# Local attention layers: one slot for both key tiles of a unit, a new queue order on ScalarE, the last norm moved into the feed-forward half, offsets added on VectorE

## The chip, the cores and the metric

The kernel runs on one core of a Trainium2 chip. The metric is the device time of one execution in microseconds (us). A core has a matrix engine (TensorE, PE in the profile, with its weight loads as PEld), VectorE (DVE), ScalarE (ACT), GpSimd (POOL) and a queue of its own for DMAs (SP). Each engine runs its own instructions in order and waits for the others by semaphores.

## The reference, cut to what matters

A network of sixteen blocks over 16 sequences of 256 tokens with 128 channels. Two of the blocks, `_L0_ffn_ref`, are made of two local layers each, so the kernel computes four local layers. One of them:

```python
def _layer(x, wqkv, qs, ksc, wo, lg, lb, w1, b1, w2, b2):
    h = shift_token(x)                     # half of the channels from the token before
    q, k, v = split(h @ wqkv)              # 8 heads of 64
    q = l2norm(q) * qs
    k = l2norm(k) * ksc
    q, k = rotary_xpos(q, k)
    # softmax over keys j with i - 64 <= j <= i, scores times 8
    o = local_attention(q, k, v)
    x = x + o @ wo
    h = shift_token(x)
    h = (h - mean(h)) / sqrt(var(h) + 1e-05) * lg + lb
    a, g = split(h @ w1 + b1)
    return x + (a * gelu(g)) @ w2 + b2
```

The performer block (`_L0_attn_b_ref`) ends its two halves with norms of the same form, with a gain and an offset.

## The kernel before, in words

The activations lie transposed, 128 channels by 4096 tokens: `x` is the residual stream, `z` (tile `ha`) a local layer's running sum, `hs` (tile `hb`) its shifted copy. A chunk is 512 tokens (two sequences; 8 chunks, `NCH`), a tile 128 tokens (32 tiles, `NTILE`).

`local_attend` handles a layer's attention. Its steps:

- `project(n)`: PE multiplies a tile of `hs` by the q and k weights into two banks of PSUM ("w"). ACT squares them into `sq`, DVE multiplies them by tables of cosines and sines into `t1` and `t2` (four products, `t<-ps,tab`).
- `rotate(n)`: DVE sums the squares (`ss`) and takes a maximum; POOL adds `t1` and `t2` crosswise (`t<-t,t`, two instructions).
- `unit(n)`: ACT turns `ss` into an inverse length (Ln, then Exp); POOL multiplies `t1` by it (`t<-t,ss`).
- `turn(n)`: PE transposes q and k (eight transposes, two "w" banks), ACT copies them into `qkt`; PE makes v (a third "w" bank), ACT copies it.
- `score`: products of keys and queries. A sequence has two tiles of keys: the first (`t` = 0) is seen by 192 queries, the second (`t` = 1) by 128. A unit is one sequence (`b`) and half of its heads (`hg`, four heads), so there are 32 units. Of the first key tile DVE masks the scores by a minimum with `see`, and ACT takes the exponential of 768 columns at once; of the second a bfloat16 product of `identb` and `masked` adds the mask on PE, and ACT takes the exponentials out of PSUM.
- `weigh`: 24 products of 32 columns: the weights' sums (`pd`, products with ones) and the weighted values (`po`). ACT then makes the inverse of `pd` (`rd`: Ln, then Exp).
- `divide`: DVE multiplies `po` by `rd` into `ot`.
- `out(c)`: four products with `wo`; DVE adds them to `z`.
- `chunk_steps`: the norm of `x` ahead of the first layer (for chunks that the stage before has not normalised already), the shifts on POOL, and for each chunk the second half's norm: `centre_step` (a PE product, ACT's copy, POOL's squares `nsq`), `spread_step` (a PE product, ACT's Ln and Exp into `nrs`), and `scale` (DVE `scalar_tensor_tensor` with the gain, ACT `Identity` with the offset).

`local_ffn` does the second half: `wide` (six products into "f" banks, Gelu on ACT, products on DVE), `narrow` (three products into a "z" bank).

The order on every engine is written out by hand (`manual_schedule`): a loop over slots `k`, two slots per key tile pair, calls the steps each with its own offset; there is no planner. Slot `k` scores one key tile of one unit and weighs the one of two slots earlier; `project` runs ten slots ahead of the tile's number times two, `out` follows ten slots later. PSUM has eight banks, shared as three "w", two "s" (scores) and three "o" (`pd` and `po`). All small operations go through helpers, so that the profile shows their lines: L504 matmul, L508 transpose, L528 ACT, L531 DVE tensor_tensor, L534 POOL, L538 and L540 DVE tensor_scalar, L543 DVE scalar_tensor_tensor; L3478 is weigh, L3406 the sum of squares.

Of the kernel before, what the change touches and what calls it, by code (L numbers as in the profile page):

```python
# [1649 lines left out]
class Fast(Net):  # L1650
# [140 lines left out]
    def norm_steps(self, pool, src, dst, bank, g=None, b=None, eps="eps5", copy=None, square=False):  # L1791


        held = {}

        def centre():
            held[0] = self.centre_step(pool, src, dst, bank, copy, square)

        def spread():
            held[1] = self.spread_step(pool, held[0], bank, eps)  # L1800

        def scale():
            if g is None:
                self.tt(dst, dst, held[1], ALU.mult)
            else:
                self.stt(dst, dst, g, held[1], ALU.mult, ALU.mult)
                self.act(dst, dst, AF.Identity, bias=b)

        return [centre, spread, scale]

# [1549 lines left out]
    def local_attend(self, w, z, hs, last):  # L3360

        nc = self.nc
        with ExitStack() as st:
            p = self.stage(st, "l1", 1)
# [9 lines left out]
            masked = one([P, P], "masked", BF16)  # L3377
            self.ts(masked, w["see"][:, :P], 0.0, ALU.min)
            identb = one([P, P], "identb", BF16)
            nc.vector.tensor_copy(identb, self.ident)  # L3380
            least = one([P, 16], "least")
            nc.gpsimd.memset(least, 1e-24)
            made, rot, qkt, val, weights, sums, outs, steps = {}, {}, {}, {}, {}, {}, {}, {}

            def project(n):
                s = slice(n * P, n * P + P)
# [26 lines left out]
            def unit(n):  # L3413
                t1, ss = rot[n]

                self.act(ss, ss, AF.Ln, scale=2.0**20)
                self.act(ss, ss, AF.Exp, scale=-0.5)
                t3 = t1.rearrange("p i h a d -> p (i h) (a d)")
                self.gt(t3, t3, ss[:, :, None].broadcast_to([P, 16, 64]), ALU.mult)
# [13 lines left out]
                val[n] = p.tile([P, 512], F32, tag="v", name="v", bufs=6)  # L3433
                self.act(val[n], pv, AF.Copy)

            def score(b, hg, t):
                wide = 192 - 64 * t
                qt, kt = qkt[b][:, 0], qkt[b][:, 1]
                ps = [self.bank("s"), self.bank("s")]
                pt = p.tile([P, 2, 384], F32, tag="pt", name="pt", bufs=4)  # L3440
                if t:
                    for a in range(2):
                        self.mm(ps[a][:, :T], identb, self.twice(masked), stop=False)
                for i in range(2):
                    g = 2 * hg + i
                    for a in range(2):
                        rows = slice(64 * a, 64 * a + 64)
                        self.mm(
                            ps[a][:, i * wide : i * wide + wide], kt[rows, g, t * P : t * P + P],
                            qt[rows, g, t * P : t * P + wide], start=t == 0, stop=t == 0 or i == 1,  # L3450
                        )
                if t:
                    for a in range(2):
                        self.act(pt[:, a, :T], ps[a][:, :T], AF.Exp)
                else:
                    for a in range(2):
                        self.tt(
                            pt[:, a].rearrange("p (i t) -> p i t", i=2), ps[a][:, :384].rearrange("p (i t) -> p i t", i=2),
                            self.twice(w["see"]), ALU.min,
                        )  # L3460
                    flat = pt.rearrange("p a t -> p (a t)")
                    self.act(flat, flat, AF.Exp)
                weights[b, hg, t] = pt

            def weigh(b, hg, t):


                wide = 192 - 64 * t
                if t == 0:
                    sums[b, hg] = self.bank("o"), self.bank("o")  # L3470
                pt = weights.pop((b, hg, t))
                pd, po = sums[b, hg]
                for half in range(-1, 2):
                    for r in range(4):
                        i, a = divmod(r, 2)
                        d = (4 * hg + r) * 64 + 32 * half
                        at = max(half, 0) * T + t * P
                        nc.tensor.matmul(  # L3478
                            (pd if half < 0 else po)[32 * r : 32 * r + 32, at : at + wide],
                            self.ones64[:, :32] if half < 0 else val[2 * b + t][:, d : d + 32],  # L3480
                            pt[:, a, i * wide : i * wide + wide], start=t == 0 and half < 1, stop=t == 1 and half != 0,
                            skip_group_check=True,
                        )
                if t == 1:
                    del sums[b, hg]
                    rd = p.tile([P, T], F32, tag="rd", name="rd", bufs=2)
                    self.act(rd, pd[:, :T], AF.Ln)
                    self.act(rd, rd, AF.Exp, scale=-1.0)
                    sums[b, hg] = po, rd

            def divide(b, hg):
                if b % 2 == 0 and hg == 0:
                    outs[b // 2] = p.tile([P, 4, CH], F32, tag="ot", name="ot", bufs=1)
                po, rd = sums.pop((b, hg))
                at = b % 2 * T
                self.tt(
                    outs[b // 2][:, 2 * hg : 2 * hg + 2, at : at + T], po.rearrange("p (g t) -> p g t", g=2),
                    self.twice(rd), ALU.mult,
                )
# [6 lines left out]
                zs = z[:, self.chunk(c)]  # L3506
                self.tt(zs, zs, pz, ALU.add)

            def at(k, slot, every, many):

                n, rest = divmod(k - slot, every)
                return n if rest == 0 and 0 <= n < many else None

            def chunk_steps(k):
                if not last:
                    for i, slot in enumerate((-17, -15, -13)):
                        if (c := at(k, slot, 8, NCH)) is not None:
                            self.norm_x_step(p, c, i, "w")
                for slot in (-12, 11):
                    if (c := at(k, slot, 8, NCH)) is not None:  # L3520
                        self.shift(hs[:, self.chunk(c)], z[:, self.chunk(c)])
                for i, slot in enumerate((12, 14, 16)):
                    if (c := at(k, slot, 8, NCH)) is not None:
                        if i == 0:
                            s = hs[:, self.chunk(c)]
                            steps[1] = self.norm_steps(p, s, s, "w", w["lg"], w["lb"])
                        steps[1][i]()

            with self.share(w=3, s=2, o=3), self.tc.manual_schedule():
                self.logs()  # L3530
                units = [(b, hg, t) for b in range(B) for hg in range(2) for t in range(2)]
                for k in range(-17, len(units) + 17):
                    if k % 2 == 0 and 0 <= k - 4 < len(units):
                        divide(*units[k - 4][:2])
                    if (n := at(k, -7, 2, NTILE)) is not None:
                        unit(n)
                    if 0 <= k < len(units):
                        score(*units[k])
                    if 0 <= k - 2 < len(units):
                        weigh(*units[k - 2])  # L3540
                    if (n := at(k, -10, 2, NTILE)) is not None:
                        project(n)
                    if (n := at(k, -9, 2, NTILE)) is not None:
                        rotate(n)
                    if (n := at(k, -5, 2, NTILE)) is not None:
                        turn(n)
                    if (c := at(k, 10, 8, NCH)) is not None:
                        out(c)
                    chunk_steps(k)

    def local_ffn(self, w, z, hn, last):
        with ExitStack() as st:
            p = self.stage(st, "l3", 2)
# [22 lines left out]

            lead = self.lead(p, "z", tables=True) if last else []
            with self.share(f=6, z=2), self.tc.manual_schedule():
                for k in range(NCH + 1 + len(lead)):
                    if k < NCH:  # L3580
                        wide(k)
                    if 0 < k <= NCH:
                        narrow(k - 1)
                    for i in reversed(range(len(lead))):
                        if 0 <= (c := k - 2 - i) < NCH:
                            lead[i](c)
# [221 lines left out]
```

## Time and profile before

| what | us |
|---|---|
| median of 3 runs (4367.05 to 4376.58) | 4374.96 |
| the profiled execution, its own time | 4392.96 |
| its span | 4391.2 |
| PE busy | 3966.2 |
| DVE busy | 2605.3 |
| ACT busy | 2376.1 |
| POOL busy | 2119.4 |
| first to last score, layers 1 to 4 | 272.8, 259.3, 272.8, 259.6 |
| unit to unit in layer 2, a repeating group of four | 7.42, 12.03, 8.28, 8.28 |

The profile is of one execution, whose time stands beside its span. In a row of the timeline the columns are the start, the time from its first to its last instruction, the engine, the line, the operation, what it writes and reads, its form, the count, and in brackets the idle time of the engine before it and what ended it. A matmul in 32-bit floats stands as two instructions. In a row of busy times by stretch come the stretch, its length, then PE, PEld, DVE, ACT and POOL with their counts, the granted clock, the DMA share and GB/s. In a group of four units one unit holds the out projection (12.03), one the centre step and one the spread step of the norm (8.28 each), and one neither (7.42).

### The profile page before, as it was taken

To read this page: it belongs to the slowest core of one execution; us is meant where nothing else is said; L and a number is where in the kernel's file an instruction comes from. 1 tells how busy PE (TensorE), PEld (TensorE's weight loads), DVE (VectorE), ACT (ScalarE), POOL (GpSimd) and SP (SyncE) were. 2 spreads that over 40 slices of the span, in tenths; PEclk is the share of its full clock that TensorE was granted. 3 is DMA by queue.
4 is the path that set the end of the run, shared out by engine and by line. 5 is a ranking of instruction groups with operands and counts; after the bars stand their busy time and mean duration, and the time that the engine had idled before them with its cause. 6 is when DMAs were issued, how large, how long until landed. Compare 5 with 4: busy or idle time off the path is not lost. (4 is left out here: it accounts for less than half of the span.)

```text
span 4391.2 us, 72802 instructions
## 1 busy us (share of the span) xinstructions
PE 3966.2 (90%) x28390; PEld 2202.4 (50%) x28390; DVE 2605.3 (59%) x4455; ACT 2376.1 (54%) x4549; POOL 2119.4 (48%) x1776
## 2 busy tenths in 40 slices
PE   7899999999899999995989969887999899899978
PEld 3455455466355445543975549643333344355333
DVE  4764566364366377456336643564888788386374
ACT  6665466444766456553447634445555554675442
POOL 4653355232455255315433334466998789521251
PEclk8999999999999999997999979998999999999989
DMA  1800000000000000001940029200000000000000
GB/s 59 332 1 1 11 1 1 19 1 1 19 1 1 1 3 1 1 0 49 310 162 10 15 88 326 86 18 16 1 1 1 3 1 1 15 2 18 6 0 20
DMA packets 78400, 176.36 MB, mean 40 GB/s; under 512 B 12606, under 2 KB 39108, under 8 KB 77920
## 3 DMA queue, kind: packets, MB, share of 16 engines
q1 hardware_dynamic: 65568, 148.40, 9.8%
q0 software_dynamic: 9120, 18.51, 1.2%
q8 instruction: 227, 3.72, 0.4%
q10 hardware_dynamic: 3360, 4.72, 0.3%
q14 instruction: 125, 1.02, 0.1%
HBM read 118.28 MB, written 54.20 MB: 39 GB/s over the span
## 5 line engine op out<-in xcount | busy, mean ns | idle before, releaser
L528 ACT ACTIVATE pt<-ps 128x512 f32<-128x512 f32 (+1 forms) x896 | 423.1, 537 | 408.1 <-PE ps L504 406.8
L504 PE MATMUL ps<-hb,w 128*128 128x512 f32 (+1 forms) x960 | 468.9, 623 | 5.4 <-issue 3.3
L531 DVE TENSOR_TENSOR t<-ps,tab 128x512 f32<-128x512 f32 x512 | 319.3, 683 | 196.1 <-ACT sq L528 191.3
L504 PE MATMUL ps<-w,hb 128*128 128x512 f32 (+2 forms) x896 | 415.1, 576 | 13.6 <-DVE t L531 11.3
L534 POOL TENSOR_TENSOR t<-t,ss 128x1024 f32<-128x1024 f32 x128 | 243.7, 1904 | 306.8 <-ACT ss L528 197.7
L534 POOL TENSOR_TENSOR t<-t,t 128x512 f32<-128x512 f32 x256 | 320.5, 1275 | 13.2 <-PE ps L504 10.1
L504 PEld LDWEIGHTS ps<-hb,w 128*128 128x128 f32 (+1 forms) x960 | 183.6, 196 | 273.5 <-issue 247.3
L531 DVE TENSOR_TENSOR u<-u,ps 128x384 f32<-128x384 f32 (+1 forms) x206 | 121.8, 595 | 277.8 <-ACT u L528 131.2
L534 POOL TENSOR_TENSOR nsq<-ha 128x512 f32<-128x512 f32 x112 | 123.2, 1100 | 314.1 <-ACT ha L528 297.3
L504 PE MATMUL ps<-nsq,ct 128*128 128x512 f32 x368 | 209.5, 654 | 53.9 <-POOL nsq L534 35.0
L528 ACT ACTIVATE pt<-pt 128x768 f32<-128x768 f32 (+1 forms) x160 | 169.5, 1060 | 154.6 <-DVE pt L531 154.6
L2199 POOL DMA_INDIRECT back<-y,x x142 | 139.1, 980 | 184.2 <-ACT y L528 90.2
L504 PE MATMUL ps<-qkt 64*128 64x192 f32 (+1 forms) x2048 | 216.2, 326 | 11.8 <-ACT pt L528 11.8
L504 PE MATMUL ps<-u,w 128*128 128x512 f32 (+1 forms) x448 | 218.8, 612 | 8.0 <-POOL u L534 8.0
L504 PE MATMUL ps<-ot,w 128*128 128x512 f32 x448 | 211.1, 604 | 15.2 <-POOL ot L534 6.9
L504 PE MATMUL ps<-xt,w 128*128 128x128 f32 x1704 | 219.8, 279 | 1.5 <-ACT xt L528 1.5
L504 PEld LDWEIGHTS ps<-qkt 64*128 64x128 f32 x2048 | 153.1, 188 | 133.3 <-ACT qkt L528 51.5
L504 PEld LDWEIGHTS ps<-w,hb 128*128 128x128 f32 x896 | 147.4, 192 | 139.4 <-issue 110.7
L531 DVE TENSOR_TENSOR pt<-ps,w 128x384 f32<-128x384 f32 (+1 forms) x320 | 171.2, 576 | 75.6 <-PE ps L504 72.2
L3705 POOL DMA_INDIRECT rows<-out,idx x128 | 126.4, 988 | 174.6 <-ACT out L528 125.6
L528 ACT ACTIVATE u<-ps,w 128x512 f32<-128x512 f32 x160 | 107.2, 685 | 186.3 <-PE ps L504 183.5
L531 DVE TENSOR_TENSOR pt<-pt,w 128x1024 f32<-128x1024 f32 (+1 forms) x96 | 181.1, 1886 | 42.3 <-ACT pt L528 42.3
(362 smaller groups left out, 9127.2 us busy)
## 6 DMA issues: line engine op xcount, KB each, us to landing
w<-in_moe_x SPq DMA_DIRECT2D x142, 533.0 KB
rows<-t SPq DMA_DIRECT2D x64, 520.0 KB
x<-rows SPq DMA_DIRECT2D x142, 65.0 KB
w<-in_local_f SPq DMA_DIRECT2D x8, 659.5 KB
y<-back ACTq DMA_DIRECT2D x16, 256.0 KB
y<-back SPq DMA_DIRECT2D x16, 256.0 KB
w<-in_local_f SPq DMA_DIRECT2D x4, 658.5 KB
back<-y,x POOLq DMA_INDIRECT x142
```

The lines of the kernel that those rows point to most:

```text
L504: self.nc.tensor.matmul(out, lhsT, rhs, start=start, stop=stop)
L528: self.nc.scalar.activation(out, in_, func, **kw)
L531: self.nc.vector.tensor_tensor(out, a, b, op)
L534: self.nc.gpsimd.tensor_tensor(out, a, b, op)
L2199: nc.gpsimd.indirect_dma_start(views[i], bass.IndirectOffsetOnAxis(ap=x[:, C : C + 1].bitcast(I32), axis=0), y, None, bounds_check=2 * NT ...
L3705: nc.gpsimd.indirect_dma_start(views[(c * 2 + k) * 4 + t], bass.IndirectOffsetOnAxis(ap=idx[:, k, t : t + 1], axis=0), out[:, k, t], None,)
```

## The change

- Both key tiles of a unit are scored in one slot and weighed in the next; the loop now runs over units `m` (32 in a layer), with one position for every step. The scores of a unit take four "s" banks; the second key tile's mask is four products of 128 columns instead of two of 256. The second tile's weights go to a tile of their own, `pu`. `pd` takes the free half of the fourth score bank of the unit that was just scored, `po` the only "o" bank: PSUM is shared as three "w", four "s", one "o".
- ACT's queue: in a unit the copies of `turn` stand ahead of the exponentials that wait for DVE's minimum (`first_weights`).
- The second half's norm (`norm_of_half`) has four steps instead of three: gain (DVE) and offset are apart, the offset now a DVE `tensor_scalar`. In DVE's queue both stand between `divide` and the products of `project`; before, the gain stood after those products. The last chunk's norm runs in `local_ffn`, one step beside each of its first four `wide` calls, with a load of the logarithm's table on ACT ahead of the second.
- `norm_steps`, which the performer uses too, adds its offset on DVE instead of ACT.

```diff
-                self.act(dst, dst, AF.Identity, bias=b)
+                self.ts(dst, dst, b, ALU.add)
...
+            def score(m):
+                b, hg = divmod(m, 2)
                 qt, kt = qkt[b][:, 0], qkt[b][:, 1]
+                ps = [self.bank("s") for _ in range(4)]
+                for x in (*(b[:, 384:] for b in ps[:2]), *(b[:, :P] for b in ps[2:])):
+                    self.mm(x, identb, masked, stop=False)
...
+                for i, t, bank, at in ((0, 0, 0, 0), (1, 0, 0, 192), (0, 1, 0, 384), (1, 1, 2, 0)):
                     for a in range(2):
+                        product(a, i, t, ps[bank + a][:, at : at + 192 - 64 * t])
+                pt = p.tile([P, 2, 384], F32, tag="pt", name="pt", bufs=2)
+                pu = p.tile([P, 4, P], F32, tag="pu", name="pu", bufs=2)
+                for a in range(2):
+                    self.tt(
+                        pt[:, a].rearrange("p (i t) -> p i t", i=2), ps[a][:, :384].rearrange("p (i t) -> p i t", i=2),
+                        self.twice(w["see"]), ALU.min,
+                    )
+                for a in range(2):
+                    self.act(pu[:, 2 + a], ps[2 + a][:, :P], AF.Exp)
+                weights[m] = pt, pu
+                spare[:] = ps
+
+            def first_weights(m):
+                pt, pu = weights[m]
+                for a in range(2):
+                    self.act(pu[:, a], spare[a][:, 384:], AF.Exp)
+                flat = pt.rearrange("p a t -> p (a t)")
+                self.act(flat, flat, AF.Exp)
+
+            def weigh(m):
+                b, hg = divmod(m, 2)
+                pd, po = spare[3][:, T:] if m < NTILE - 1 else self.bank("s")[:, T:], self.bank("o")
+                pt, pu = weights.pop(m)
+                for half in (0, 1, -1):
+                    for t in range(2):
...
-            with self.share(w=3, s=2, o=3), self.tc.manual_schedule():
+            with self.share(w=3, s=4, o=1), self.tc.manual_schedule():
                 self.logs()
...
+                for m in range(-9, NTILE + 6):
+                    if within(m, NTILE):
+                        score(m)
+                    if within(m - 1, NTILE):
+                        weigh(m - 1)
+                    c, rest = divmod(m - 5, 4)
+                    if rest == 0 and 0 <= c < NCH:
                         out(c)
+                    if within(m + 2, NTILE):
+                        turn(m + 2)
+                    if within(m, NTILE):
+                        first_weights(m)
+                    if within(m + 4, NTILE):
+                        rotate(m + 4)
+                    if within(m - 1, NTILE):
+                        inverse(m - 1)
+                        divide(m - 1)
+                    if within(m + 4, NTILE):
+                        unit(m + 4)
+                    chunk_steps(m)
+                    if within(m + 5, NTILE):
+                        project(m + 5)
+
+    def norm_of_half(self, pool, bank, w, s):
+        held = {}
+        def centre():
+            held[0] = self.centre_step(pool, s, s, bank)
+        def spread():
+            held[1] = self.spread_step(pool, held[0], bank)
+        return [
+            centre, spread, lambda: self.stt(s, s, w["lg"], held[1], ALU.mult, ALU.mult),
+            lambda: self.ts(s, s, w["lb"], ALU.add),
+        ]
...
             with self.share(f=6, z=2), self.tc.manual_schedule():
+                end = self.norm_of_half(p, "z", w, hn[:, self.chunk(NCH - 1)])
                 for k in range(NCH + 1 + len(lead)):
                     if k < NCH:
                         wide(k)
+                    if k < 4:
+                        if k == 1:
+                            self.logs(False)
+                        end[k]()
```

In a group of four units the new loop puts `out`, a POOL shift and the offset of the chunk before into the first, the other shift and the centre step into the second, the spread step into the third, and the gain into the fourth. For chunks 5 to 7 of layers 1 and 3 the steps of the norm of `x` fall into the third, fourth and first.

More of the change, by code (lines that the diff above doesn't have):

```diff
@@ L3382, in local_attend @@
             nc.gpsimd.memset(least, 1e-24)
-            made, rot, qkt, val, weights, sums, outs, steps = {}, {}, {}, {}, {}, {}, {}, {}
+            made, rot, qkt, val, weights, sums, outs, steps, spare = {}, {}, {}, {}, {}, {}, {}, {}, []
             def project(n):
@@ L3434, in turn @@
                 self.act(val[n], pv, AF.Copy)
-            def score(b, hg, t):
-                wide = 192 - 64 * t
+            def score(m):
+                b, hg = divmod(m, 2)
                 qt, kt = qkt[b][:, 0], qkt[b][:, 1]
-                ps = [self.bank("s"), self.bank("s")]
-                pt = p.tile([P, 2, 384], F32, tag="pt", name="pt", bufs=4)
-                if t:
-                    for a in range(2):
[L3443 to L3489, printed above, removed]
@@ L3491, in divide, with product @@
-            def divide(b, hg):
-                if b % 2 == 0 and hg == 0:
+                ps = [self.bank("s") for _ in range(4)]
+                for x in (*(b[:, 384:] for b in ps[:2]), *(b[:, :P] for b in ps[2:])):
+                    self.mm(x, identb, masked, stop=False)
+                def product(a, i, t, out):
+                    rows, g = slice(64 * a, 64 * a + 64), 2 * hg + i
+                    wide = 192 - 64 * t
+                    nc.tensor.matmul(
+                        out, kt[rows, g, t * P : t * P + P], qt[rows, g, t * P : t * P + wide],
+                        start=False, stop=True, skip_group_check=t == 0,
+                    )
@@ new lines, in score @@
+                for i, t, bank, at in ((0, 0, 0, 0), (1, 0, 0, 192), (0, 1, 0, 384), (1, 1, 2, 0)):
+                    for a in range(2):
+                        product(a, i, t, ps[bank + a][:, at : at + 192 - 64 * t])
[5 more added lines that the diff above has]
+                        self.twice(w["see"]), ALU.min,
+                    )
@@ new lines, in score @@
+                for a in range(2):
[14 more added lines that the diff above has]
+                    for t in range(2):
+                        wide = 192 - 64 * t
+                        for r in range(4):
+                            i, a = divmod(r, 2)
+                            d = (4 * hg + r) * 64 + 32 * half
+                            at = max(half, 0) * T + t * P
+                            nc.tensor.matmul(
+                                (pd if half < 0 else po)[32 * r : 32 * r + 32, at : at + wide],
+                                self.ones64[:, :32] if half < 0 else val[2 * b + t][:, d : d + 32],
+                                pu[:, r] if t else pt[:, a, i * wide : i * wide + wide],
+                                start=t == 0 and half < 1, stop=t == 1 and half != 0, skip_group_check=True,
+                            )
+                sums[m] = pd, po
@@ L3493, in divide, with inverse @@
+            def inverse(m):
+                pd, po = sums[m]
+                rd = p.tile([P, T], F32, tag="rd", name="rd", bufs=2)
+                self.act(rd, pd, AF.Ln)
+                self.act(rd, rd, AF.Exp, scale=-1.0)
+                sums[m] = po, rd
+            def divide(m):
+                b, hg = divmod(m, 2)
+                if m % 4 == 0:
                     outs[b // 2] = p.tile([P, 4, CH], F32, tag="ot", name="ot", bufs=1)
-                po, rd = sums.pop((b, hg))
+                po, rd = sums.pop(m)
@@ L3507, in out, with within, chunk_steps, due @@
                 self.tt(zs, zs, pz, ALU.add)
[L3509 to L3514, printed above, removed]
+            def within(n, many):
+                return 0 <= n < many
+            def chunk_steps(m):
+                def due(slot):
+                    c, rest = divmod(m - slot, 4)
+                    return c if rest == 0 and 0 <= c < NCH else None
                 if not last:
-                    for i, slot in enumerate((-17, -15, -13)):
-                        if (c := at(k, slot, 8, NCH)) is not None:
+                    for i in range(3):
+                        if (c := due(i - 9)) is not None:
@@ L3518, in chunk_steps @@
                             self.norm_x_step(p, c, i, "w")
-                for slot in (-12, 11):
-                    if (c := at(k, slot, 8, NCH)) is not None:
+                for slot in (-6, 5):
+                    if (c := due(slot)) is not None:
                         self.shift(hs[:, self.chunk(c)], z[:, self.chunk(c)])
-                for i, slot in enumerate((12, 14, 16)):
-                    if (c := at(k, slot, 8, NCH)) is not None:
+                for i in range(4):
+                    if (c := due(6 + i)) is not None and c < NCH - 1:
@@ L3524, in chunk_steps @@
                         if i == 0:
-                            s = hs[:, self.chunk(c)]
-                            steps[1] = self.norm_steps(p, s, s, "w", w["lg"], w["lb"])
+                            steps[1] = self.norm_of_half(p, "w", w, hs[:, self.chunk(c)])
                         steps[1][i]()
-            with self.share(w=3, s=2, o=3), self.tc.manual_schedule():
+            with self.share(w=3, s=4, o=1), self.tc.manual_schedule():
                 self.logs()
[L3531 to L3547, printed above, removed]
-                        out(c)
-                    chunk_steps(k)
```

## The prediction

> **What bounds the kernel now.** I read the page's first part, then the busy time of a repeating stretch of 36 us, then TensorE's timeline inside it. The page says that TensorE (PE) is busy for 90% of the span.
>
> ```profile
> PE 3966.2 (90%) x28390; PEld 2202.4 (50%) x28390; DVE 2605.3 (59%) x4455; ACT 2376.1 (54%) x4549; POOL 2119.4 (48%) x1776
> ```
>
> One group in layer 2 (a chunk of 512 tokens: four units of two sequences, one out projection, one norm):
>
> ```profile
> 596.00:632.00 36.00, 35.16 (x333) 20.23 (x332) 25.09 (x39) 23.37 (x54) 21.04 (x19) 1.00 0.01 2
> ```
>
> PE is busy 35.16 of 36.00, the others under 70%. Its rows of one unit (8.28 us, 602.35 to 610.63), and the one gap of the group:
>
> ```profile
> 602.35 0.92 PE L504 MATMUL ps<-qkt 64*128 64x192 f32 x8
> 603.20 0.53 PE L3478 MATMUL ps<-pt,ct 128*32 128x192 f32 x8
> 603.55 0.83 PE L3478 MATMUL ps<-pt,v 128*32 128x192 f32 x16
> 604.32 1.98 PE L504 MATMUL ps<-w,hb 128*128 128x512 f32 x4
> 606.14 1.02 PE L504 MATMUL ps<-hb,ct 128*128 128x512 f32 x2
> 607.00 0.38 PE L504 MATMUL ps<-masked,identb 128*128 128x256 bf16 x2
> 607.31 0.71 PE L504 MATMUL ps<-qkt 64*128 64x128 f32 x8
> 607.95 0.43 PE L3478 MATMUL ps<-pt,ct 128*32 128x128 f32 x8
> 608.20 0.62 PE L3478 MATMUL ps<-pt,v 128*32 128x128 f32 x16
> 608.75 1.09 PE L508 MATMUL ps<-ct,t 128*128 128x128 f32 x8
> ...
> 627.23 1.19 PE L504 MATMUL ps<-qkt 64*128 64x192 f32 x8 [0.84 <-ACT pt L528]
> ```
>
> Start to start, a 192-wide score block takes 0.85 and a 128-wide one 0.64; the weigh blocks 1.12 and 0.80. Inside a block, four or six slots of 0.163 us (192) or 0.109 us (128) follow each other, by the start times of single products; so 0.1 to 0.2 us per block is lost where the tile form (64*128, 128*32, 128*128) changes. The gap at 627.23 makes one unit in four 1.18 us longer; its cause stands in ACT's queue:
>
> ```profile
> 625.06 0.74 DVE L543 SCALAR_TENSOR_TENSOR hb<-hb,w,nrs 128x512 f32<-128x512 f32 x1
> 625.84 0.72 ACT L528 ACTIVATE hb<-hb,w 128x512 f32<-128x512 f32 x1 [2.35 <-DVE hb L543]
> 626.82 0.64 ACT L528 ACTIVATE pt<-ps 128x256 f32<-128x256 f32 x2
> ```
>
> The offset (Identity) waits 2.35 us for DVE, and the exponentials behind it free the score banks late. The end of a layer is a chain instead, with PE at half clock (products 0.86 apart, not 0.43):
>
> ```profile
> 423.65 1.45 PE L504 MATMUL ps<-ot,w 128*128 128x512 f32 x3
> 427.33 1.43 PE L504 MATMUL ps<-hb,ct 128*128 128x512 f32 x2 [2.23 <-POOL hb L696]
> 430.56 2.07 PE L504 MATMUL ps<-nsq,ct 128*128 128x512 f32 x2 [1.81 <-POOL nsq L534]
> 432.43 3.95 PE L504 MATMUL ps<-hb,w 128*128 128x512 f32 x6
> ```
>
> [...]the same operations take 0.345 and 0.73 us alone, and far longer over a POOL instruction:
>
> ```profile
> L538 DVE TENSOR_SCALAR qz<-q,ct x96: 336/345/1424, 2288.4 to 3989.0; 128x256 f32<-128x256 f32 x96
> L543 DVE SCALAR_TENSOR_TENSOR hb<-ha,w,nrs x32: 726/780/2659, 21.4 to 4163.0; 128x512 f32<-128x512 f32 x32
> ```
>
> [...]
>
> **The change, part by part** (times in us).
>
> 1. *Seams.* Both key tiles in one slot: a unit has three tile forms in a row instead of six. Saved: score 128 (0.64-0.44), weigh 128 (0.80-0.65), project (1.82-1.72): 0.45. Masks keep their columns (2x256 to 4x128) but load identb four times (98 ns each): 0 to +0.2; I take +0.0. A plain unit's PE work falls from 7.42 to 6.97.
>
> 2. *A loop takes the seams back.* All four s banks are now one unit's, and the fourth also holds the pd of the unit before. In the built program's semaphores the fourth mask therefore waits for ACT's Ln of pd, and behind that mask stands PE's whole queue. That Ln stands behind everything that ACT does for the unit: copies of the transposes and of v, then the first weights' Exp. From mask to mask: scores 1.19 and seam 0.17, weigh 1.65 and seams 0.21, eight transposes 0.93, v product to its end 1.02, then ACT's v copy 0.04+0.48, two Exp of 128 columns 0.38 (no such row; the 256-wide take 0.377 and start 0.28 apart; 0.36 to 0.50), Exp of 768 0.76, Ln 0.39, semaphore 0.05. Sum 7.27, say 7.3 (7.2 to 7.5). That is above 6.97: a plain unit gains 0.12. With a norm product (0.86, outside the loop) PE rules: 8.28 to 7.82. The out unit (3.43 inside the loop) goes from 12.03 to 7.3+3.43=10.73: the 1.18 gap goes with the Identity.
>
> 3. *Offsets and scales ahead of the rotations on VectorE.* In the program's order stt, ts (and ha*nrs of the x norm) now stand between divide and project's four products on DVE. Divide ends 0.7 after rd's Exp; by then ss's Exp is done too and POOL has begun t*ss (1.90)[...]. Behind ts on DVE stand project's four t products, and for them wait PE, by two w banks, and POOL's t+t. ts (no such row: 0.35, the half-size qz, to 0.74, an stt; I take 0.6) waits about 1.7 (its turn comes at 8.5 after the unit's start, t*ss runs from 8.3 to 10.3, the out projection's 3.4 left aside), and the four t products (0.6 each) end 2.3 later. They free the two w banks that the next unit's second transposes and v product need: v at 6.1 instead of 4.4 after that unit's start. The centre unit becomes 7.82+1.7=9.5. stt does the same a unit earlier, but there the 3.43 of out covers it. The four t products themselves[...] last 0.68 over POOL as without it. In the spread unit ACT has nrs (0.72+0.54) ahead of its squares, so the next unit's Exp on the fourth bank, and with it pd's products, come about 0.25 late: 7.6. ts hidden: 0; not: 1.7.
>
> Group: 10.73+9.5+7.82+7.6=35.65, before 36.01.
>
> 4. *Whole attention*, first to last score. Layers 2 and 4: 6.6 (first unit) + 4x7.3 + 33.97 (first group, no ts yet) + 4x35.65 + 10.73+9.5+2x7.3+10.73+4.3 = 262.2, before 259.3: +2.9. The last units have no project, so the loop costs most there. Layers 1 and 3 normalise x for three chunks; my group is 37.7 (two products of 0.86[...]), so 268.4 against 272.8: -4.4; their gaps behind the Identity go.
>
> 5. *The last norm beside the first FFN products.* Before, from the last unit's first score to FFN at full clock: 19.6 (413.7 to 433.2 in layer 1, counting four products at half clock as 1.7 lost). After: score 1.6, wait for the pt and po of the last two units until 5.2, weigh 1.65, out in two halves 3.5 around divide: 10.4 to 11.3, plus the moved products 2x0.86 in FFN: 12.4. Saved 7.2 a layer. ACT's copy, Ln, Exp and two more table loads (1.28 each), POOL's nsq, DVE's stt and ts lie beside FFN products, where ACT is busy 13.5 of 50; uncovered they would cost 2.6 a layer.
>
> 6. *Nothing:* the performer's 16 offsets on DVE (its FFN has PE 25.00 of 25.00; ±0.7 each at an end). The start: unit's Ln now precedes the next squares, 5.1 per projection instead of 4.5, but one transposition fewer stands ahead of the first score: ±1 a layer. No step that moves issues a DMA.
>
> Sum: 2x(2.9-7.2)+2x(-4.4-7.2) = -32 on the profiled execution's 4392.96. That execution lies 18 above the median of the runs, 4374.96; I take the difference over: **4343**.
>
> **Rivals.** (a) *The whole seam gain.* If [...]ACT's chain is shorter than 6.97, PE rules: groups of 33.0, attention about 242 and 247, 24 to 33 less per layer: about 4260. For it: PE is the busiest by far. Against: the chain's durations are measured. 0.22. (b) *Slower: the loop through ACT and the banks.* The same fourth bank and the single o bank, with unpriced start gaps of 0.1 on eight steps, make every unit about 0.5 longer than I have it: 31x4x0.5=+62, so +30: 4405. It decides from 0.26 a unit on. For it: three of my waits have less than 0.4 of slack (pd 0.1 to 0.5, v bank 0.35, o bank 0.3), where before three w, two s, three o banks left slack. Against: before, ACT's start gaps are the 0.03 to 0.05 that I used. 0.26. (c) That the slot isn't merged: out, the built order shows twelve score products in a row.
>
> **How the numbers follow.** The likeliest case, 0.52, has 4310 to 4372 ([...]loop 7.2 to 7.5, end 5 to 8). About 0.2% (8.7 us) is what a measurement here can tell from no change. Faster: 0.46 of it and 0.22 of (a), 0.68; same: 0.06, and 0.05 of (b); slower 0.21. The range leaves out the ends of (a) and (b): 4262 to 4398.
>
> **What would show it.** Right: plain units at 7.3 with PE waiting before a mask for ACT's rd; out units at 10.7 without a gap; ts at 1.5 to 2.3 us over POOL, and a wait for DVE's t before the v product one unit later; no half clock ahead of FFN. Wrong: units of 7.0 (a), units over 7.8 or waits before weigh for ot (b), a gap at FFN's start.

## The result, and the profile after

The changed kernel takes 4332.51 us (median of 4 runs, 4325.84 to 4336.18), the kernel before 4375.77 beside it: a ratio of 0.9903, interval 0.9884 to 0.9922. That is 43 us less (34 to 51). The forecast was 4343, 32 less.

The two profiled executions are 67 us apart in their spans (4391.2 and 4323.9), more than the medians. By stage, before to after, in us (for the four layers in their order where there are four numbers; the last score is the first one of a layer's last unit, and the narrow product is the feed-forward half's second step):

| stretch | before | after | sum |
|---|---|---|---|
| first to last score of a layer | 272.8, 259.3, 272.8, 259.6 | 273.1, 261.6, 271.5, 261.6 | +3.3 |
| last score to first narrow product | 30.2 each | 23.2 each | -28.0 |
| feed-forward's end to the first score, layers 2 and 4 | 24.4, 24.7 | 22.7, 22.6 | -3.9 |
| layer 2's feed-forward to layer 3's first score (holds the performer) | 329.0 | 319.9 | -9.1 |
| start to layer 1's first score | 140.9 | 136.3 | -4.6 |
| layer 4's feed-forward to the next feed-forward, untouched | 1601.8 | 1578.8 | -23.1 |
| the rest | | | -1.9 |

The row of -23 holds no line of the change. In the later profiles, of kernels that have the same lines there, it takes 1578 to 1586 on the chip on which the kernel before took 4373, and 1601 to 1605 on the two on which it took 4397 and 4394: it goes with the chip. That the profiles of before and after come from different chips fits this, but isn't on record. A second profile of the changed kernel has the start at 141.2, so the -4.6 isn't the change's either. What repeats in that second profile is +3.3, -28, -4 and -9, together -38; the last of these depends on the granted clock (experiment 5).

Busy times of a group of four units in layer 2, 567.31 to 602.77, after:

```profile
567.31:602.77 35.46, 34.12 (x343) 21.25 (x342) 27.16 (x40) 22.09 (x61) 21.30 (x19) 1.00 0.01 1
```

35.46, where the group before took 36.0; but TensorE (PE) is now idle 1.3 of it. Unit by unit it is 7.64, 10.84, 9.23 and 7.75. TensorE's timeline in a plain unit, one without an out projection or a norm product (7.19, from mask to mask 518.80 to 525.98), and ACT's beside it:

```profile
518.80 0.69 PE L504 MATMUL ps<-masked,identb 128*128 128x128 bf16 x4
519.41 1.36 PE L3449 MATMUL ps<-qkt 64*128 64x192 f32 x16
520.71 0.53 PE L3489 MATMUL ps<-pt,v 128*32 128x192 f32 x8
...
522.48 1.09 PE L508 MATMUL ps<-ct,t 128*128 128x128 f32 x8
523.40 2.74 PE L504 MATMUL ps<-w,hb 128*128 128x512 f32 x6
525.98 0.69 PE L504 MATMUL ps<-masked,identb 128*128 128x128 bf16 x4
```

```profile
524.96 0.44 ACT L528 ACTIVATE pu<-ps 128x128 f32<-128x128 f32 x2
525.27 0.85 ACT L528 ACTIVATE pt<-pt 128x768 f32<-128x768 f32 x1
526.01 0.40 ACT L528 ACTIVATE rd<-ps 128x256 f32<-128x256 f32 x1
```

All of a unit's scores and all of its weighing now lie together, three tile forms in a row. The four masks take 0.69, spread out: the fourth starts only when ACT's Ln of the sums (rd<-ps, 526.01 to 526.41) has ended. The wait is short, since TensorE's own work is almost as long as that loop.

### The profile page after: what moved, and what is told of

It reads as the page before. It is cut to its first block, busy times and chain, and to the rows that moved or that the text cites. A ratio compares the mean times of both kernels' runs of the same rounds, so it can differ in the third digit from the quotient of the medians.

```text
span 4323.9 us, 73393 instructions
## 1 busy us (share of the span) xinstructions
PE 3902.5 (90%) x28646; PEld 2230.1 (52%) x28646; DVE 2661.6 (62%) x4503; ACT 2341.3 (54%) x4765; POOL 2127.3 (49%) x1776
## 5 line engine op out<-in xcount | busy, mean ns | idle before, releaser
L528 ACT ACTIVATE pt<-ps 128x512 f32<-128x512 f32 x640 | 339.8, 601 | 313.0 <-PE ps L504 311.8
L504 PE MATMUL ps<-w,hb 128*128 128x512 f32 (+2 forms) x896 | 406.0, 575 | 32.6 <-DVE t L531 26.4
L528 ACT ACTIVATE qkt<-ps 128x512 f32<-128x512 f32 x256 | 142.0, 595 | 330.4 <-PE ps L508 329.8
L531 DVE TENSOR_TENSOR ot<-ps,rd 128x512 f32<-128x512 f32 (+1 forms) x208 | 136.5, 656 | 255.1 <-ACT rd L528 253.2
L504 PEld LDWEIGHTS ps<-w,hb 128*128 128x128 f32 x896 | 157.5, 194 | 194.7 <-issue 109.5
L504 PEld LDWEIGHTS ps<-xt,w 128*128 128x128 f32 x1704 | 203.8, 193 | 3.3 <-ACT xt L528 3.3
L534 POOL TENSOR_TENSOR both<-pt 128x1024 f32<-128x1024 f32 x64 | 169.7, 2651 | 44.5 <-DVE pt L531 28.8
```

The source lines that it names most:

```text
L504: self.nc.tensor.matmul(out, lhsT, rhs, start=start, stop=stop)
L528: self.nc.scalar.activation(out, in_, func, **kw)
L531: self.nc.vector.tensor_tensor(out, a, b, op)
L534: self.nc.gpsimd.tensor_tensor(out, a, b, op)
```

## The experiments

The three sets ran on chips on which the kernel before took 4397, 4373 and 4394, so ratios to it are compared; 0.001 is 4.4 us. The changed kernel was measured beside the second set and gave 0.9906 there, 0.9903 in the first result. A difference of two ratios carries both their intervals, some 8 to 10 us.

**1. Where VectorE's three norm operations stand.** Three kernels, each against the changed one. `s_ahead` calls the steps that multiply and add (gain, offset, and the x norm's scale) ahead of the inverse, the other steps where they were:

```diff
+                    chunk_steps(m, True)
                     if within(m - 1, NTILE):
                         inverse(m - 1)
                         divide(m - 1)
...
-                    chunk_steps(m)
+                    chunk_steps(m, False)
                     if within(m + 5, NTILE):
                         project(m + 5)
```

> The three DVE operations of the norms that stand between divide and the products of project (gain, offset, and the scale of the x norm) are moved in DVE's queue ahead of the wait for rd, behind the maximum of rotate. Nothing else moves. Theory[...]: POOL is idle there between its two kinds of work, so the offset takes about 0.5 us instead of 2.04 and the gain 0.74 instead of 2.30; the unit with the centre step falls from 9.23 to 7.75, a group in layers 2 and 4 from 35.46 to about 34.0, these layers by about 9 each, layers 1 and 3 by 9 to 15 each; time about 4285 to 4297. Rival (the centre step's own product, copy and squares make that unit long, or VectorE's sheer load does): the operations may get shorter but the unit stays near 9.2 and the time within 10 of 4332.

Measured: ratio 0.9816 (0.9803 to 0.9829), 38 us under the changed kernel. Units with the centre step fell from 9.23 to 7.75, groups to 33.98, layer 2 from 261.6 to 254.3 (7 less, where 9 was expected), layer 1 from 273.1 to 259.0. The offset's instances, first of the changed kernel, then of this one (durations in ns: least, median, most):

```profile
L538 DVE TENSOR_SCALAR hb<-hb,w x40: 473/658/2040, 216.6 to 1842.4; 128x512 f32<-128x512 f32 x40
```

```profile
L538 DVE TENSOR_SCALAR hb<-hb,w x40: 472/480/491, 219.8 to 1808.4; 128x512 f32<-128x512 f32 x40
```

The 2040 of the first row is seen in the changed kernel's timelines of DVE, of POOL and then of PE, one unit later:

```profile
586.07 0.69 DVE L531 TENSOR_TENSOR ot<-ps,rd 128x512 f32<-128x512 f32 x1 [2.30 <-ACT rd L528]
586.68 2.04 DVE L538 TENSOR_SCALAR hb<-hb,w 128x512 f32<-128x512 f32 x1
588.64 2.47 DVE L531 TENSOR_TENSOR t<-ps,tab 128x512 f32<-128x512 f32 x4
```

```profile
586.53 1.90 POOL L534 TENSOR_TENSOR t<-t,ss 128x1024 f32<-128x1024 f32 x1 [3.35 <-ACT ss L528]
```

```profile
589.97 0.66 PE L508 MATMUL ps<-ct,t 128*128 128x128 f32 x4 [0.46 <-DVE t L531]
591.16 1.12 PE L504 MATMUL ps<-w,hb 128*128 128x512 f32 x2 [0.54 <-DVE t L531]
```

POOL's multiplication began 0.15 ahead of the offset and ran until 588.43. The offset, 0.48 by itself, ends at 588.72, only 0.29 behind POOL's end. All 14 offsets that begin 0.15 behind that multiplication take 2.04, and the longest of the other 26 takes 0.83; in `i_first` below, where some offsets begin 0.32 ahead of it, they take 0.48. The products t<-ps,tab behind the offset come late, the w banks they read stay taken, and TensorE waits twice. Moving three instructions, with nothing removed, takes the wait away. The rival (the centre step's own work) falls.

`s_behind` calls the same steps behind `project`, where the gain stood before the change:

```diff
                     if within(m + 5, NTILE):
                         project(m + 5)
+                    chunk_steps(m, True)
```

> The same three DVE operations moved behind the four products of project, where the gain stood in the kernel before. Theory: project's products are on time again, so the centre unit falls to between 7.75 and 8.3; but the operations now meet POOL's t+t (two of 1.25), and what stands behind them is the minimum of the next scores, so some of it comes back: 10 to 36 us under the changed kernel, 4296 to 4322. Rival (the centre step's own work, or VectorE's load): the unit stays near 9.2 and the time near 4332.

Measured: 0.9823 (0.981 to 0.9836), 35 less. In layer 2 as good as `s_ahead` (groups of 33.96), though the offset meets POOL's t<-t,t there and takes up to 1.49: no product that TensorE waits for stands behind it. In layers 1 and 3, with the x norm's scale in the same place, centre units are 8.38 and those layers 4 longer than in `s_ahead`.

`s_act` has the offset on ACT again, at its new place one unit behind the gain:

```diff
-            lambda: self.ts(s, s, w["lb"], ALU.add),
+            lambda: self.act(s, s, AF.Identity, bias=w["lb"]),
```

> The local norm's offset is an Identity on ACT again, in the slot where the changed kernel has it on DVE (one slot after the gain). Theory[...]: no offset stands ahead of project's products on DVE, so the centre unit falls from 9.23 to about 7.75; ACT's 0.72 ahead of the squares makes it or the one behind it up to 0.5 longer; groups 34.0 to 34.6, 5 to 9 less a layer, 4296 to 4312. Its input is a whole unit old, so there is no wait of 2.35 as in the kernel before. Rival (the centre step's own work): 9.2 stays, and ACT's 0.72 is added to it; 4332 or above.

Measured: 0.9852 (0.9838 to 0.9865), 22 less. Centre units 8.12 in layer 2, groups 34.34; 9.5 in the later groups of layers 1 and 3, where the x norm's scale still stands behind divide. As the theory had it.

**2. The loop through the fourth bank.** `i_first` takes the inverse out from between rotate and divide and puts it ahead of the first weights:

```diff
+                    if within(m - 1, NTILE):
+                        inverse(m - 1)
                     if within(m, NTILE):
                         first_weights(m)
```

> On ACT the inverse of the sums of the unit before (Ln and Exp) stands ahead of the exponentials of the first weights, not behind them. Theory (loop through the fourth score bank): the fourth mask no longer waits for it; plain units go from 7.19 to TensorE's own 7.05 and the gap of 0.14 ahead of a mask goes; the unit behind the spread step from 7.64 to 7.2 to 7.5. Divide comes about 1.2 earlier as well, so that gain and offset behind it are done before POOL's t*ss begins: offset near 0.5, centre unit 7.75. Together groups of 33.5 to 33.9, time 4280 to 4296. Rival (the loop runs through the exponentials themselves, not through the bank of the sums): plain units stay at 7.19 or get 0.5 longer, since the first weights come 0.7 later[...].

Measured: 0.9765 (0.9752 to 0.9779), 60 us under the changed kernel, where 36 to 52 was expected, and 103 under the one before: the best of all kernels here. Plain units take 6.96 (expected 7.05), out units 10.56, the group 33.46. The same group of four units, and a plain unit's masks with ACT ahead of them:

```profile
553.29:586.75 33.46, 33.40 (x343) 21.26 (x341) 24.33 (x39) 21.97 (x61) 21.11 (x19) 1.00 0.01 1
```

```profile
518.86 0.38 ACT L528 ACTIVATE rd<-ps 128x256 f32<-128x256 f32 x1
519.27 0.42 ACT L528 ACTIVATE rd<-rd 128x256 f32<-128x256 f32 x1
519.59 0.43 ACT L528 ACTIVATE pu<-ps 128x128 f32<-128x128 f32 x2
519.91 0.85 ACT L528 ACTIVATE pt<-pt 128x768 f32<-128x768 f32 x1
```

```profile
519.88 0.41 PE L504 MATMUL ps<-masked,identb 128*128 128x128 bf16 x4
```

TensorE is busy 33.40 of 33.46; four masks take 0.41 instead of 0.69, since Ln is done 0.6 ahead of them. No offset waits for POOL any more (longest 0.49): divide comes earlier, so one move takes away both waits. The plain units tell the loop from the wait for POOL: no norm operation stands in the first ones of a layer, `s_ahead` leaves them at 7.19, and only this move brings them to 6.96.

**3. What a change of tile form costs.** On `i_first`, the weighing is cut in two: two of its three parts stay, the second value half goes behind the transposes and v. That adds two changes of form and no work.

```diff
                     if within(m - 1, NTILE):
-                        weigh(m - 1)
+                        weigh(m - 1, (-1, 0))
...
                         turn(m + 2)
+                    if within(m - 1, NTILE):
+                        weigh(m - 1, (1,))
```

> Against the kernel with the inverse first (plain units 6.96, bound by TensorE alone): weigh is cut in two, and the second value half stands behind the transposes and v, which makes two changes of the tile form more per unit and changes no work. Theory (each change costs 0.1 to 0.2, as read from the starts in the kernel before): plain units 7.2 to 7.35, 25 to 50 slower than the kernel with the inverse first (ratio 0.9765), ratio 0.982 to 0.988. Rival (changes cost nothing, the saving came from fewer waits): units at 6.96 to 7.0, ratio 0.976 to 0.978.

Measured: 0.9975 (0.9964 to 0.9985), far outside what was expected: plain units 7.82. The trace shows why. With the sums (-1) first, TensorE writes the fourth bank right behind the scores and waits 0.53 for ACT to read the scores in it. Only the other 0.33 can be the form. Hence `seams2`, with (0, -1) in place of (-1, 0):

> The kernel with the inverse first, weigh cut in two as in the run before, but with a value half ahead of the sums, so that TensorE does not come to the bank of the sums before ACT has read the scores in it (0.53 of the 0.86 that each unit was longer). Theory (two more changes of the tile form, 0.165 each): plain units 7.29 to 7.4, first to last score of layer 2 up by 9 to 13 from 248.4; ratio 0.983 to 0.988. Rival (most of the 0.86 is not the form): units of 7.6 or more with no wait shown.

Measured: 0.9815 (0.9802 to 0.9829), 22 above `i_first`; plain units 7.28. Its plain unit:

```profile
524.88 1.09 PE L508 MATMUL ps<-ct,t 128*128 128x128 f32 x8
525.80 1.02 PE L504 MATMUL ps<-w,hb 128*128 128x512 f32 x2
526.76 0.53 PE L3491 MATMUL ps<-pt,v 128*32 128x192 f32 x8
527.11 0.40 PE L3491 MATMUL ps<-pu,v 128*32 128x128 f32 x8
527.44 1.98 PE L504 MATMUL ps<-w,hb 128*128 128x512 f32 x4
```

No waits, the same products, 0.32 more: 0.16 for each change of form. Layer 2 is 6.2 longer, less than the 9 to 13 expected, because not every unit is TensorE's: those behind the spread step stay (7.33 and 7.36), and the last, without project, get shorter.

**4. The end of a layer.** `n_end_inside` puts the last chunk's norm back into attention:

```diff
-                    if (c := due(6 + i)) is not None and c < NCH - 1:
+                    if (c := due(6 + i)) is not None:
...
-                for m in range(-9, NTILE + 6):
+                for m in range(-9, NTILE + 10):
...
-                    if k < 4:
-                        if k == 1:
-                            self.logs(False)
-                        end[k]()
```

> The changed kernel with the last chunk's norm inside attention again, ahead of the first feed-forward product, as in the kernel before. Theory (the end of a layer is a chain of engines, with TensorE at half clock): the stretch from the last score to the first narrow product is about 7 longer in each of four layers, 30.2 instead of 23.2; the whole 26 to 30 slower than the changed kernel. Rival (the end got shorter through the single slot, the norm would be hidden in part): under 12 slower.

Measured: 0.9939 (0.9926 to 0.9953), 13 us over the changed kernel beside it (4346.89 and 4333.83): neither theory's number. By the trace the stretch is 28.5, 28.3, 29.8 and 29.9 instead of 23.2, so 5.1 to 6.7 a layer and 24 in all. The ratios' difference, 0.0033, or 14 us, is uncertain by some 9, so the 24 lies at its edge; what else made this kernel's runs shorter stays open. The same move on the kernel before (`b_both` below) is 23 by the traces and 22 by the times. Of the 7.0 a layer, the norm's place is then about 5.9. The other 1.1 is the single slot's for the most part: the centre product begins 12.7 behind the last score instead of 13.6. Here is layer 1's end with the norm inside, then as changed:

```profile
418.24 3.73 PE L504 MATMUL ps<-ot,w 128*128 128x512 f32 x8
424.39 1.12 PE L504 MATMUL ps<-hb,ct 128*128 128x512 f32 x2 [2.43 <-POOL hb L696]
427.32 2.08 PE L504 MATMUL ps<-nsq,ct 128*128 128x512 f32 x2 [1.80 <-POOL nsq L534]
429.19 11.15 PE L504 MATMUL ps<-hb,w 128*128 128x512 f32 x24
```

```profile
415.96 3.73 PE L504 MATMUL ps<-ot,w 128*128 128x512 f32 x8
420.47 5.42 PE L504 MATMUL ps<-hb,w 128*128 128x512 f32 x12 [0.78 <-DVE ha L531]
425.73 1.02 PE L504 MATMUL ps<-hb,ct 128*128 128x512 f32 x2
426.58 5.31 PE L504 MATMUL ps<-hb,w 128*128 128x512 f32 x12
431.74 1.02 PE L504 MATMUL ps<-nsq,ct 128*128 128x512 f32 x2
```

Two waits of 2.4 and 1.8 go, and the two products lie among others. In the first view the second pair of products takes 2.08, in the second 1.02. There twelve instructions take 5.42, 0.43 apart, where at half clock, in the kernel before (432.43), they are 0.85 apart; the granted clock from 409.40 to 432.60 is 1.00: the end is at full clock.

**5. The performer's offset.** `p_offset_act` undoes only the line in `norm_steps`; `after_again` is the changed kernel beside it.

```diff
-                self.ts(dst, dst, b, ALU.add)
+                self.act(dst, dst, AF.Identity, bias=b)
```

> The changed kernel with the performer's offset on ACT again (norm_steps), nothing else. As predicted (no effect beyond 0.7 at each of its ends): within 3 of the changed kernel. Rival (ACT's offset stood in the chain at the performer's ends, where the stage between layers 2 and 3 lost 9 and the first one 4.6 in the changed kernel's profile): 4 to 10 slower than the changed kernel, all of it ahead of the first scores of layers 1 and 3.

> The changed kernel itself, for comparison with the others on this chip: a ratio of 0.990 to the kernel before, the same periods of the units (7.19, 10.84, 9.23, 7.64, 7.75).

Measured: 0.9921 (0.9908 to 0.9935) against 0.9906 (0.9891 to 0.9921), medians 4338.65 and 4333.83. The intervals overlap, so the times alone don't decide it. The traces do better: from layer 2's feed-forward to layer 3's first score it is 327.5 with the offset on ACT (before: 329.0), and 315.6 to 324.3 in the eleven profiles with it on DVE. The place, first with ACT's offset (ACT, then PE), then changed:

```profile
1055.93 0.72 ACT L528 ACTIVATE hb<-hb,w 128x512 f32<-128x512 f32 x1 [0.89 <-DVE hb L543]
1056.56 0.58 ACT L528 ACTIVATE ot<-ps 128x512 f32<-128x512 f32 x1
```

```profile
1057.19 1.25 PE L504 MATMUL ps<-ot,w 128*128 128x512 f32 x2 [2.68 <-ACT ot L528]
```

```profile
1053.00 2.08 PE L504 MATMUL ps<-ot,w 128*128 128x512 f32 x2 [1.07 <-ACT ot L528]
```

It is the local layers' gap once more: an Identity that waits for DVE's gain, and behind it in ACT's queue the copy that the last products need. Here it is worth 1.6 (2.68 against 1.07). The profiles also differ in how long this stretch runs at half clock, from 17 us to 41 (before 37.5, after 34.1). `i_first`, which has the offset on DVE, spends 41.0 there as `p_offset_act` does and takes 322.5, so the offset's part is 5.0: 1.6 here and 3.4 between here and layer 3's first score.

**6. Parts alone on the kernel before.** `b_offset` changes that one line of the kernel before (so in local layers and performer); `b_both` also moves the last norm among the feed-forward products.

```diff
-                self.act(dst, dst, AF.Identity, bias=b)
+                self.ts(dst, dst, b, ALU.add)
```

> The kernel before with one line changed: the offset of norm_steps on DVE (tensor_scalar) instead of ACT, in the local layers and in the performer. Theory (the Identity that waits 2.35 for DVE holds up the exponentials behind it and costs 1.18 in one unit of four, and at the performer's ends it holds up the copies of the outputs): groups in layer 2 fall from 36.0 to about 34.8, layers 2 and 4 by 6 to 7, layers 1 and 3 by 7 to 14, the performer's end ahead of layer 3 by 5 to 8; together 28 to 45 less, ratio 0.990 to 0.994, as much as the whole change brought. Rival (the gap has another cause, or the offset on DVE meets POOL's t+t and delays the minimum as much): groups stay at 35.6 to 36.2, at most 10 less in all.

> The kernel before with the offset on DVE and the last chunk's norm moved among the first feed-forward products; slots, banks and ACT's order stay as before. Theory: the parts add up, 5 to 7 per layer from the end on top of the offset's gain: ratio 0.984 to 0.989, 48 to 70 less than before, better than the whole changed kernel (0.990). Then the merged slot with gain and offset behind divide cost more than it brought. Rival (the end's gain needs the single slot): ratio as with the offset alone.

Measured: 0.9878 (0.9863 to 0.9894) and 0.9827 (0.9814 to 0.984). One line brings 53 us (46 to 60), at least as much as the whole change with its 43 (34 to 51). Layer 2 falls to 253.4, layer 1 to 260.4, as TensorE has no gap left in a group:

```profile
512.80:547.60 34.80, 34.80 (x354) 20.08 (x343) 27.30 (x42) 23.18 (x53) 21.14 (x17) 1.00 0.01 2
```

The expectation was 28 to 45: I had left out that the layers' ends get shorter too (last score to first narrow product 28.6, 29.3, 29.7 and 29.3 instead of 30.2), 4 in all; the traces then add up to 46 (37 in the attentions, 5 ahead of layer 3, 4 at the ends). With the norm moved the ends are 23.4, and 22 us more come off: the parts add up, to 76 instead of the 48 to 70 expected. So the merged slot as it was put, with VectorE's operations behind divide and the inverse behind the exponentials, gave back 34 us (0.9827 to 0.9903). With the inverse first it brings 27 beyond `b_both` (0.9827 to 0.9765).

## Why the prediction was right, and where its terms were off

The four mechanisms that it names (the seams, the loop through ACT, VectorE's wait over POOL, the chain at a layer's end) are all in the traces, at nearly the sizes it gave. That the sum came as near as it did is in part luck, as the last three points show.

- *What bounds the kernel.* TensorE, and one ACT wait per group: right. `b_offset` removes that wait alone and gets 34.80 of 34.80.
- *Step 1, seams.* TensorE's own plain unit was put at 6.97 with 0.1 to 0.2 for a change of form; `i_first` shows 6.96, `seams2` 0.16 for one change, whatever it is made of.
- *Step 2, the loop.* Forecast 7.3, measured 7.19; out units 10.73 and 10.84. `i_first` shows that it was the order on ACT: without it 6.96 and 10.56.
- *Step 3, VectorE over POOL.* Forecast: offset 2.3 over POOL, centre unit 9.5, next units 7.82 and 7.6, group 35.65. Measured: 2.04, 9.23, 7.75, 7.64, 35.46. Of the 2.3, the wait of 1.7 was an estimate. That the products t<-ps,tab last as long over POOL also holds: of the changed kernel's 512, the 152 that lie over POOL's instructions alone take 0.68 (median; longest 0.69), the 188 over none as well.
- *Step 4.* Layers 2 and 4: 262.2 forecast, 261.6 measured. Layers 1 and 3 are the miss: -4.4 each forecast, +0.2 and -1.3 measured. For the groups with the x norm the forecast has one number, 37.7; layer 1 has 37.3, then 38.7, 40.4 and 38.5. DVE and PE in such a unit of layer 1:

```profile
292.94 2.30 DVE L531 TENSOR_TENSOR ha<-ha,nrs 128x512 f32<-128x512 f32 x1
295.17 0.83 DVE L538 TENSOR_SCALAR hb<-hb,w 128x512 f32<-128x512 f32 x1
```

```profile
297.25 0.66 PE L508 MATMUL ps<-ct,t 128*128 128x128 f32 x4 [1.47 <-DVE t L531]
298.44 2.07 PE L504 MATMUL ps<-w,hb 128*128 128x512 f32 x2 [0.54 <-DVE t L531]
300.31 1.79 PE L504 MATMUL ps<-hb,ct 128*128 128x512 f32 x2
```

  The scale takes the wait for t<-t,ss (2.30, where over no POOL instruction it is 0.68) and the offset then waits for POOL's shift (0.83, by itself 0.48), so the products start 2.9 after divide's end instead of 1.9. That takes the unit from 9.23 to 10.25; where TensorE falls to half clock behind its wait, as here (1.87 for two products, not 0.86), it is 11.9. `s_ahead` brings these units to 7.75.
- *Step 5.* Saved 7.2 a layer forecast, 7.0 measured, of which the norm's place is about 5.9. The half clock at the end goes, as forecast. In the kernel before, TensorE was busy 1.18 in the 3.41 ahead of the fall, and its longest wait was 2.23. That stretch and the next, at half clock:

```profile
424.62:428.03 3.41, 1.18 (x4) 0.30 (x2) 0.69 (x1) 0.00 (x0) 1.31 (x3) 1.00 0.00 0
428.03:431.44 3.41, 1.60 (x2) 0.50 (x2) 0.00 (x0) 0.60 (x1) 1.04 (x1) 0.50 0.00 0
```

- *Step 6.* Costed at nothing, and wrong: the performer's ends gave 5 to 9, the starts of layers 2 and 4 some 2 each, and for these no run shows the cause. I had looked at the performer's feed-forward, where TensorE is full, and not at the queue behind the Identity at its end. The miss in step 4 (+8 in layers 1 and 3) makes up for more than half of this -13. The sum was to be -32; it is -38 by the stages that repeat and -43 (34 to 51) by the medians.
- *Rivals.* (a) doesn't hold as changed, but its unit of 7.0 is what `i_first` reaches. (b) asked for 0.26 more per unit than my 7.3; units came in 0.1 below it.

## What to carry to other kernels

Ask of an operation moved to VectorE not only what it costs but what stands behind it in the queue, and which GpSimd instruction starts just then: here three instructions cost 38 us more at one place than a few instructions earlier, in VectorE's own wait. When banks are merged, the last read of each bank joins the chain of the next unit, so put that read first in its engine's queue. And test the parts alone: one line of this change was worth at least as much as all of it.

## What was not expected of the hardware

TensorE fell to half clock without being idle for a microsecond at a time. In the last units of a layer there is no project, and behind two gaps of 0.8 in a unit the granted clock fell:

```profile
749.89 0.39 PE L504 MATMUL ps<-masked,identb 128*128 128x128 bf16 x2 [0.80 <-ACT pu L528]
751.07 0.22 PE L504 MATMUL ps<-masked,identb 128*128 128x128 bf16 x1 [0.79 <-ACT rd L528]
751.21 1.42 PE L3449 MATMUL ps<-qkt 64*128 64x192 f32 x16
752.56 0.87 PE L3489 MATMUL ps<-pt,v 128*32 128x192 f32 x8
```

The last row takes 0.87, in the full units 0.53, and the unit 12.46 instead of 10.84. The clock fell at 752.39 and rose again 3.41 later. Here are the stretch ahead, which holds both gaps, and the one at half clock:

```profile
748.98:752.39 3.41, 1.82 (x21) 1.36 (x18) 0.89 (x2) 2.35 (x6) 0.00 (x0) 1.00 0.00 0
752.39:755.80 3.41, 3.41 (x52) 2.17 (x48) 1.39 (x3) 0.45 (x2) 0.00 (x0) 0.50 0.02 5
```

In all thirteen traces half clock lasts 3.41 us or a multiple of it (but for the record that a trace ends in), so the clock can be set against how busy TensorE was in the 3.41 us ahead. Of such stretches at full clock, from TensorE's first instruction on, half clock followed all 414 in which it was busy under 40%, 168 of the 518 between 40% and 60%, and 4 of some 12000 over 90%; in the two traces of before and after alone it followed all 68, 24 of 87 and 1 of 1846. The stretch above is 53% busy, and in other layers and runs of these kernels stretches about as busy did not bring the fall. So in these traces the fall came behind gaps of 0.8 as it did behind waits of 2.2; what decides between two stretches about as busy, they don't show.
